# Two layers of cross attention on one core: nine slots for two units in place of ten, with maxima of up to 384 queries in a slot's four PSUM banks

## The chip, the cores and the metric

The kernel runs on one core of one Trainium2 chip. The metric is the device time of one execution in microseconds (us), and lower is better. All arithmetic is in fp32. The profile is of one execution on the same core.

## The reference, cut to what matters

Two cross-attention layers stand one behind the other. There are 32 batches of 256 queries with 320 channels, a context of 77 rows of 512 channels for each batch, and 20 heads of 16 channels. The context is so short that the object, adapter and image parts of the two original layers are empty; what is left is the same computation twice, with different weights:

```
q   = x @ Wq                    # (32, 256, 320)
k,v = ctx @ Wk, ctx @ Wv        # (32, 77, 320)
s   = q_h . k_h / 4             # per head h, 256 x 77
p   = softmax(s over the 77 keys)
x   = (merge_h(p @ v_h)) @ Wo + b + x
```

The second layer takes the x that the first has made.

## The kernel before, in words

**Layout.** Channels stand on partitions. A pair of batches (`NB = 2`) is one tile of x, 128 partitions by 1280 columns: channels 0 to 127 and 128 to 255 of both batches, and the last 64 channels of the two batches below each other. One pair in one layer is a *unit*; there are 32 units. `units_in_order` gives layer 0 of the first four pairs, and then layer 1 of a pair and layer 0 of a later pair in turn, so that from unit 4 on the even units are layer 1 and the odd ones layer 0.

**Groups.** The heads of a unit are worked on in five *groups* g of 256 queries (`of_group`): a group has eight heads of one batch, two in each of the four strips of 32 partitions (j = 0 to 3).

**Steps of a unit u**, each a function:

- `queries` with `queries_rest`, or, from unit 3 on, `outputs_and_queries(u - 3, u)`: the output projection of an older unit and the query projection of this one in one long step. Its results are added to x by VectorE (`add`, L520) and copied to the tile q0 by ScalarE (L369, L372), in the order rest, group 0, 1, 2, 3. A DMA copies q0 to q1.
- `keys(u, 0)`, `keys(u, 1)`, `keys_rest(u)`: the key projection, copied by ScalarE, masked for even and odd heads by GpSimd (`mask_keys`, tiles kT). `less_keys` makes the tile kM from the same keys.
- `vals` and `place_vals`: value projection in chunks of 128 context rows, copied by ScalarE and placed by DMA.
- `maxima(u, g)` (L423, tiles psm): the scores of the 256 queries of a group with all keys, queries on partitions. Each of the four strips has its own PSUM bank with 2 x 154 columns; VectorE reduces each bank to the maxima (L431). A call is 8 matmuls in the code, 16 in the profile[...].
- `turn(u)` (L440): VectorE transposes the maxima of the unit, and eight small DMAs write them into free rows of q0 and q1. These rows make the matmul of the scores take the maximum off.
- `scores(u, g)` (L458, tiles pss): keys on partitions, four banks of 512 columns, and ScalarE's exponential of each bank into a tile pT (L464).
- `values(u, g)` (L478, tile po): the product with the values, one bank; then `divide`: VectorE transposes the bank (L490) and takes reciprocals (L494), GpSimd multiplies (L499).
- `turn_back(u, g)` (L513): VectorE transposes the group back into the tile oT, from which the output projection reads.

Matmuls with 32 rows (psm, pss) use TensorE as four row tiles; those with 32 output channels (po and all projections) as four column tiles, and a few with 64 rows as eight tiles.

**Order.** All instructions are issued in an order written out by hand. `place` maps a slot number and a name to steps; the slots are walked one after the other, and in a slot the names in this order:

```
order = (
    "load", "maxima", "turn", "turn back", "scores", "values", "rest", "back", "full", "last",
)
```

Each engine works its instructions off in that order; only semaphores hold it up. Before, unit u has its groups in slots `NG * u` to `NG * u + 4`: one group of scores, one of values and one call of maxima in each slot, the long step `outputs_and_queries` in every fifth slot. PSUM has one pool of eight banks for everything (`bank`), which are given out in turn: a tile gets the bank of the tile eight allocations earlier, and has to wait until that one has been read. In the last units (`late`) the output projection is cut in two halves (`finish(u, (t,))`, which reads group 4 of oT first) and `finish_rest`, to fill slots that have no other work.

Of the kernel before, what the change touches and what calls it, by code (L numbers as in the profile page):

```python
# [52 lines left out]
B, S, C, CA, L = 32, 256, 320, 512, 77  # L56
HEADS, HD = 20, 16
P = 128
# [4 lines left out]
NG = 5  # L63
# [29 lines left out]
def xattn_kernel(ctx: ExitStack, tc: tile.TileContext, xT, cT, cP, weights, outT):  # L93
# [2 lines left out]
    const = ctx.enter_context(tc.tile_pool(name="const", bufs=1))  # L96
    io = ctx.enter_context(tc.tile_pool(name="io", bufs=3))
    work = ctx.enter_context(tc.tile_pool(name="work", bufs=3))
    probs = ctx.enter_context(tc.tile_pool(name="probs", bufs=8))
    psum = ctx.enter_context(tc.tile_pool(name="psum", bufs=8, space=bass.MemoryType.PSUM))  # L100

    units = units_in_order()
    NU = len(units)

    def bank(name):
        return psum.tile([P, 512], F32, tag="bank", name=name)
# [3 lines left out]
    def load_x(p):  # L110
        x_sb = io.tile([P, NX], F32, tag="x", name=f"x_{p}", bufs=AHEAD + 3)
        xs[p] = x_sb
        if p == 0:
            for a, b in ((0, NT), (NT, 2 * NT), (2 * NT, NX)):
                nc.sync.dma_start(out=x_sb[:, a:b], in_=xT[p, :, a:b])
        else:
            (nc.scalar if p == 1 else nc.sync).dma_start(out=x_sb, in_=xT[p])

    def load_context(u):
        p = units[u][0]  # L120
        c_sb = cs[u] = io.tile([P, NKA, NB * L], F32, tag="c", name=f"c_{u}", bufs=3)
        nc.sync.dma_start(out=c_sb, in_=cP[:, p])
# [18 lines left out]
    first, _, _ = PARTS["q"]  # L141
# [50 lines left out]
    def of_group(x, g):  # L192

        if g < 4:
            return x[:, (g // 2) * NT + (g % 2) * S : (g // 2) * NT + (g % 2 + 1) * S]
        return x[:, 2 * NT : NX]
# [75 lines left out]
    def keys(u, t):  # L272
        p, layer = units[u]
        w, c_sb = w_sb[layer], cs[u]
        if t == 0:
            st[u]["kr"] = work.tile([P, NG, L], F32, tag="kR", name=f"kR_{u}", bufs=2)
        kR = st[u]["kr"]
        ps = bank(f"psk_{u}_{t}")
        for kc in range(NKA):
            by_columns(  # L280
                ps[:, 0 : 2 * L],
                w["k"][:, kc, t * P : (t + 1) * P],
                c_sb[:, kc, :],
                start=(kc == 0),
                stop=(kc == NKA - 1),
            )
        nc.scalar.copy(kR[:, 2 * t : 2 * t + 2].rearrange("p g k -> p (g k)"), ps[:, 0 : 2 * L])  # L287
        mask_keys(u, t)

    def keys_rest(u):  # L290

        p, layer = units[u]
        w, c_sb = w_sb[layer], cs[u]
        ps = bank(f"psk_{u}_2")
        for kc in range(NKA):
            for i in range(4):
                b, m = 1 - i // 2, i % 2
                nc.tensor.matmul(  # L298
                    ps[32 * i : 32 * i + 32, 0:L],
                    w["k"][:, kc, 2 * P + 32 * m : 2 * P + 32 * m + 32],  # L300
                    c_sb[:, kc, b * L : (b + 1) * L],
                    start=(kc == 0),
                    stop=(kc == NKA - 1),
                )
        nc.scalar.copy(st[u]["kr"][:, 4], ps[:, 0:L])
        mask_keys(u, 2)
# [7 lines left out]
    def queries(u):  # L314

        p, layer = units[u]
        w = w_sb[layer]
        q0 = new_queries(u)
        ps = [[bank(f"psq_{u}_{t}_{b}") for b in range(NB)] for t in range(2)]
        if u == 0:  # L320

            main_channels(ps, w["q"], xs[p], start=True, stop=False)
            last_channels(ps, w["q2"], xs[p], start=False, stop=True)
        else:
            last_channels(ps, w["q2"], xs[p], start=True, stop=False)
            main_channels(ps, w["q"], xs[p], start=False, stop=True)
        for g in range(4):
            nc.scalar.copy(of_group(q0, g), ps[g // 2][g % 2][:, 0:S])

    def queries_rest(u):  # L330
        p, layer = units[u]
        w = w_sb[layer]
        q0, q1 = st[u]["q"]
        ps = bank(f"psq_{u}_2")
        project_rest(ps, w["q"], w["q22"], xs[p], swap=1)
        nc.scalar.copy(of_group(q0, 4), ps[:, 0:S])
        nc.sync.dma_start(out=q1, in_=q0)
# [75 lines left out]
                )  # L413


    def maxima(u, g):
        q0, kT, mx = st[u]["q"][0], st[u]["k", g // 2], maxes[u % 2]
        q = of_group(q0, g)
        ps = [bank(f"psm_{u}_{g}_{j}") for j in range(4)]
        for c in range(S // P):  # L420
            for j in range(4):
                r = slice(32 * j, 32 * j + 32)
                nc.tensor.matmul(  # L423
                    ps[j][:, c * 2 * L : (c + 1) * 2 * L],
                    q[r, c * P : (c + 1) * P],
                    kT[r, :, g % 2, :],
                    start=True,
                    stop=True,
                )
        for j in range(4):  # L430
            nc.vector.tensor_reduce(  # L431
                mx[:, 2 * g : 2 * g + 2, 2 * j : 2 * j + 2],
                ps[j][:, : 4 * L].rearrange("p (c e k) -> p c e k", e=2, k=L),
                AX.X,
                ALU.max,
            )
# [70 lines left out]
    def values(u, g):  # L507
        st[u]["n", g] = divide(u, g, products(u, g))
# [47 lines left out]
    def at(slot, where, step):  # L556
        place.setdefault((slot, where), []).append(step)

    end = NG * NU
    late = {
        NU - 4: (end - 10, end - 9, end - 8),
        NU - 3: (end - 7, end - 6, end - 5),
        NU - 2: (end - 4, end - 1, end - 3),
    }
    made = [0, 0]
    for u, (p, layer) in enumerate(units):
        s = NG * u
        if layer == 0 and u > 0:  # L570
            at(s - 15, "load", lambda p=p: load_x(p))
        if u > 0:
            at(s - 13, "load", lambda u=u: load_context(u))
        if u > 1:
            at(s - 9, "rest", lambda u=u: keys(u, 0))
            at(s - 9, "rest", lambda u=u: keys_rest(u))
            at(s - 8, "rest", lambda u=u: keys(u, 1))
        paired = u > 2 and u - 3 not in late
        if paired:
            at(s - 10, "full", lambda u=u: outputs_and_queries(u - 3, u))  # L580
        else:
            if u > 1:
                at(s - 10, "last", lambda u=u: queries(u))
            at(s - 6, "rest", lambda u=u: queries_rest(u))
        at(s - 6, "rest", lambda u=u: less_keys(u))
        need = range(p * NB * L // P, ((p + 1) * NB * L - 1) // P + 1)
        new = [i for i in need if i >= made[layer]]
        made[layer] += len(new)
        slots = {}
        for k, i in enumerate(new):  # L590
            at(s - 10 + k, "load", lambda layer=layer, i=i: load_chunk(layer, i))
            for h in range(2):
                slots[i] = s - 7 + (u == 0) + (k if len(new) > 1 else h)
                at(slots[i], "full", lambda layer=layer, i=i, h=h: vals(layer, i, h))
        for i in need:
            at(slots.get(i, s - 7), "full", lambda u=u, i=i: place_vals(u, i))
        for g in range(NG):
            if u > 0:
                at(s - 7 + g, "maxima", lambda u=u, g=g: maxima(u, g))
            at(s + g, "scores", lambda u=u, g=g: scores(u, g))  # L600
            at(s + g + 1, "values", lambda u=u, g=g: values(u, g))
            if g < 4:
                at(s + g + 2, "turn back", lambda u=u, g=g: turn_back(u, g))
            else:
                at(s + g + 1, "back", lambda u=u, g=g: turn_back(u, g))
        if u > 0:
            at(s - 3, "turn", lambda u=u: turn(u))
        if u == NU - 1:
            at(s + NG, "full", lambda u=u: finish(u))
            at(s + NG, "last", lambda u=u: finish_rest(u))  # L610
        if u in late:
            for t in range(2):
                at(late[u][t], "full", lambda u=u, t=t: finish(u, (t,)))
            at(late[u][2], "rest", lambda u=u: finish_rest(u))
            at(max(late[u]), "last", lambda u=u: store(u))
# [3 lines left out]
    for u, slot in ((0, -9), (1, -4)):  # L619
        for t in range(2):  # L620
            at(slot, "rest", lambda u=u, t=t: keys(u, t))
        at(slot, "rest", lambda u=u: keys_rest(u))
    for slot, g in ((-6, 0), (-5, 1), (-4, 2), (-4, 3), (-3, 4)):
        at(slot, "maxima", lambda g=g: maxima(0, g))
    at(-3, "turn", lambda: turn(0))
    at(-3, "last", lambda: queries(1))


    at(-10, "load", lambda: load_weights(0, "v", "v", nc.scalar))
# [108 lines left out]
```

## Time and profile before

| | |
|---|---|
| time, median of three executions | 961.7 us (961.33, 961.7, 3365.69) |
| the profiled execution: its time | 960.31 us |
| the profiled execution: span from first to last instruction | 958.5 us |
| granted TensorE clock | 1.000 |
| TensorE matmuls | 953.5 us busy, 20910 instructions |
| VectorE | 553.1 us busy, 1323 instructions |
| ScalarE | 435.6 us busy |
| GpSimd | 254.1 us busy |
| DMA | 83.77 MB, mean 87 GB/s |

The profile's ends of matmuls are modelled, so their durations overlap; what a phase of matmuls takes is read from the start of one phase to the start of the next. Where a fence shows lines of the timeline, the columns are start in us, duration in us, engine, line, operation, output and input tiles, shapes, number of instructions, and in brackets the idle time before with its releaser. Lines with "xcount" are groups: busy time, mean ns of one, idle time before and what ended it.

### The profile page before, as it was taken

Reading aid. Unit: us, or ns where it says so; the run is one execution under the profiler, and the core shown is the slowest. Engines: PE = TensorE matmul, PEld = TensorE weight load, DVE = VectorE, ACT = ScalarE, POOL = GpSimd, SP = SyncE. Lnnn points to the kernel's source line nnn. Section 1 sums busy time; section 2 is a strip of 40 time slices with the busy share of each in tenths; the row PEclk is TensorE's granted clock in tenths of the full one; section 3 lists DMA queues with packets and bytes.
Section 4 is the critical chain, followed back from the end, with each engine's and each line's share of the span. In section 5 each row is a group of like instructions: output and inputs, shape, how many; then the busy total and the mean of one; then the engine's idle time right before and its main releaser. Section 6 shows DMA issues by size and latency. Waiting matters only on the chain.

```text
span 958.5 us, 46529 instructions
## 1 busy us (share of the span) xinstructions
PE 953.5 (99%) x20910; PEld 628.8 (66%) x20910; DVE 553.1 (58%) x1323; ACT 435.6 (45%) x977; POOL 254.1 (27%) x422
## 2 busy tenths in 40 slices
PE   9999999999999999999999999999999999999998
PEld 7666766666666676666666666666667666667654
DVE  3456554666555665555665556655566555565664
ACT  2345544455444454444544444543445444445543
POOL 2223321333222332322332223322133222233311
PEclk9999999999999999999999999999999999999999
DMA  7533222131222222231222222322313122122102
GB/s 253 196 109 100 71 70 97 61 100 60 87 97 86 74 83 78 94 110 59 73 85 88 99 73 70 102 80 90 97 61 106 61 81 71 59 73 71 53 32 84
DMA packets 54537, 83.77 MB, mean 87 GB/s; under 512 B 15620, under 2 KB 36228, under 8 KB 54338
## 3 DMA queue, kind: packets, MB, share of 16 engines
q1 hardware_dynamic: 53386, 78.29, 25.1%
q8 instruction: 164, 2.69, 1.2%
q10 hardware_dynamic: 952, 2.50, 0.7%
q14 instruction: 35, 0.29, 0.1%
HBM read 35.39 MB, written 10.49 MB: 48 GB/s over the span
## 4 chain that ended last, share of the span: by engine, by line
PE 99%; issue 0%; DVE 0%
PE po L478 17%; PE psy L190 15%; PE psq L190 15%; PE pss L458 15%; PE psm L423 12%; PE psv L190 9%; PE psk L190 7%; PE psy L224 4%; PE psq L224 4%; PE psk L298 2%; PE warm L183 0%; DVE x L520 0%; DVE ones L150 0%
## 5 line engine op out<-in xcount | busy, mean ns | idle before, releaser
L464 ACT ACTIVATE pT<-pss 77x512 f32<-77x512 f32 x640 | 326.8, 590 | 216.4 <-PE pss L458 216.4
L431 DVE TENSOR_REDUCE max<-psm 128x4 f32<-128x308 f32 x640 | 261.5, 471 | 262.5 <-PE psm L423 262.3
L499 POOL TENSOR_TENSOR normal<-turned,inv 128x256 f32<-128x256 f32 x160 | 99.2, 620 | 678.8 <-DVE inv L494 678.8
L478 PE MATMUL po<-pT,v 77*32 77x256 f32 x2560 | 171.5, 385 | 0.0
L458 PE MATMUL pss<-q,kM 32*77 32x256 f32 x2560 | 167.1, 374 | 0.0
L190 PE MATMUL psy<-oT,w 128*32 128x256 f32 (+1 forms) x3072 | 164.4, 379 | 0.0
L190 PE MATMUL psq<-x,w 128*32 128x256 f32 (+1 forms) x3072 | 151.2, 379 | 0.0
L423 PE MATMUL psm<-kT,q 32*128 32x154 f32 x2560 | 129.6, 314 | 0.6 <-issue 0.6
L190 PEld LDWEIGHTS psy<-oT,w 128*32 128x32 f32 (+1 forms) x3072 | 88.3, 108 | 63.5 <-issue 16.1
L478 PEld LDWEIGHTS po<-pT,v 77*32 77x32 f32 x2560 | 67.0, 109 | 87.1 <-DVE max L431 56.8
L490 DVE STREAM_TRANSPOSE turned<-po 128x512 f32<-128x512 f32 x160 | 113.4, 709 | 15.3 <-PE po L478 15.3
L190 PEld LDWEIGHTS psq<-x,w 128*32 128x32 f32 (+1 forms) x3072 | 85.6, 109 | 54.0 <-issue 1.8
L423 PEld LDWEIGHTS psm<-kT,q 32*128 32x128 f32 x2560 | 92.3, 183 | 41.5 <-issue 29.5
L520 DVE SCALAR_TENSOR_TENSOR x<-psy,w,x 128x256 f32<-128x256 f32 x160 | 69.3, 478 | 81.6 <-PE psy L190 80.3
L261 POOL TENSOR_SCALAR kT<-kR,masks 128x154 f32<-128x154 f32 (+1 forms) x186 | 111.0, 612 | 9.4 <-ACT kR L287 9.4
L458 PEld LDWEIGHTS pss<-q,kM 32*77 32x77 f32 x2560 | 98.8, 141 | 19.8 <-issue 1.2
L190 PE MATMUL psv<-w,cv 128*32 128x160 f32 x2464 | 98.8, 299 | 0.0
L369 ACT COPY q<-psq 128x256 f32<-128x256 f32 x28 | 10.4, 372 | 184.5 <-PE psq L224 184.5
L190 PEld LDWEIGHTS psv<-w,cv 128*32 128x32 f32 x2464 | 82.4, 110 | 14.6 <-issue 0.5
L513 DVE STREAM_TRANSPOSE oT<-normal 128x256 f32<-128x256 f32 x160 | 68.9, 431 | 26.1 <-POOL normal L499 26.1
L190 PE MATMUL psk<-c,w 128*32 128x154 f32 x2048 | 78.8, 294 | 0.0
L190 PEld LDWEIGHTS psk<-c,w 128*32 128x32 f32 x2048 | 66.2, 110 | 11.8 <-DMA w<-in_w_dram 0.4
(31 smaller groups left out, 445.3 us busy)
## 6 DMA issues: line engine op xcount, KB each, us to landing
q<-q SPq DMA_DIRECT2D x32, 640.0 KB
c<-in_cP_dram SPq DMA_DIRECT2D x32, 308.0 KB
cv<-in_cT_dram SPq DMA_DIRECT2D x38, 256.0 KB
out_dram<-x SPq DMA_DIRECT2D x15, 640.0 KB
x<-in_xT_dram SPq DMA_DIRECT2D x14, 640.0 KB
v<-stage SPq DMA_DIRECT2D x26, 192.5 KB
q<-mT SPq DMA_DIRECT2D x254, 5.0 KB
w<-in_w_dram ACTq DMA_DIRECT2D x2, 640.0 KB
```

The source lines that it names most:

```text
L190: nc.tensor.matmul(out[m : m + 32], lhsT[:, m : m + 32], rhs, **flags)
L224: nc.tensor.matmul(ps[o : o + 32, 0:S], lhsT, rhs, **flags)
L261: engine.tensor_scalar_mul(kT[:, e], kR[:, groups], masks[:, e : e + 1])
L423: nc.tensor.matmul(ps[j][:, c * 2 * L : (c + 1) * 2 * L], q[r, c * P : (c + 1) * P], kT[r, :, g % 2, :], start=True, stop=True,)
L431: nc.vector.tensor_reduce(mx[:, 2 * g : 2 * g + 2, 2 * j : 2 * j + 2], ps[j][:, : 4 * L].rearrange("p (c e k) -> p c e k", e=2, k=L), AX.X ...
L458: nc.tensor.matmul(ps[j][:L, e * S : (e + 1) * S], kM[r, e, g, :], q[r, :], start=True, stop=True,)
L464: nc.scalar.activation(st[u]["p", g][j][:L], ps[j][:L], AF.Exp, scale=SCALE)
L478: nc.tensor.matmul(po[o : o + 32, e * S : (e + 1) * S], vpad[:L, b, pair, e].rearrange("p a d -> p (a d)"), pT[j][:L, e * S : (e + 1) * S] ...
L490: nc.vector.transpose(turned[:, 0 : 2 * S], po)
L499: nc.gpsimd.tensor_tensor(normal.rearrange("p q e d -> p e q d"), outs, inv.unsqueeze(3).broadcast_to([P, 2, S // 32, HD]), ALU.mult,)
L513: nc.vector.transpose(of_group(st[u]["o"], g), normal)
L520: nc.vector.scalar_tensor_tensor(x, ps[:, 0:S], w_sb[layer]["b"][:, 0, t : t + 1], x, ALU.add, ALU.add)
```

## The change

Two units, an even and the odd one behind it, now share nine slots in place of ten. `start(u)` is the first slot of a unit: 9k for the even unit 2k, 9k + 4 for the odd unit 2k + 1. The even unit has the scores of its groups 0 and 1 both in its first slot. `maxima` takes a run of 128-query pieces instead of a group: up to three of them (384 queries, 462 columns of a bank) go into one set of four banks and are reduced by one instruction per bank. A unit has four calls, of 1, 3, 3 and 3 pieces for an even unit and 3, 3, 2 and 2 for an odd one, in the four slots behind the slot of its query projection; that slot of an even unit has no maxima. The pool of the probabilities grows from 8 to 11 tiles. Keys, values, context and x loads, `turn` and the late outputs move with the new slots; unit 1 has all its maxima ahead of slot 0, where before they lay in slots -2 to 2.

For reference, the light work of the nine slots of a pair, with units 2k and 2k + 1 in scores and values and the next pair 2k + 2 and 2k + 3 in preparation:

| slot | maxima pieces | scores, group | values, group | projections |
|---|---|---|---|---|
| 9k | none | 2k: 0 and 1 | 2k-1: 4 | outputs 2k-1, queries 2k+2 |
| 9k+1 | 1 | 2k: 2 | 2k: 0 and 1 | keys_rest |
| 9k+2 | 3 | 2k: 3 | 2k: 2 | keys 0, vals |
| 9k+3 | 3 | 2k: 4 | 2k: 3 | keys 1, vals |
| 9k+4 | 3, then turn | 2k+1: 0 | 2k: 4 | outputs 2k, queries 2k+3 |
| 9k+5 | 3 | 2k+1: 1 | 2k+1: 0 | keys_rest, vals |
| 9k+6 | 3 | 2k+1: 2 | 2k+1: 1 | vals |
| 9k+7 | 2 | 2k+1: 3 | 2k+1: 2 | keys 0 |
| 9k+8 | 2, then turn | 2k+1: 4 | 2k+1: 3 | keys 1 |

```diff
-    probs = ctx.enter_context(tc.tile_pool(name="probs", bufs=8))
+    probs = ctx.enter_context(tc.tile_pool(name="probs", bufs=11))
...
-    def maxima(u, g):
-        q0, kT, mx = st[u]["q"][0], st[u]["k", g // 2], maxes[u % 2]
-        q = of_group(q0, g)
-        ps = [bank(f"psm_{u}_{g}_{j}") for j in range(4)]
-        for c in range(S // P):
+    def maxima(u, first, n):
+
+        q0, mx = st[u]["q"][0], maxes[u % 2]
+        ps = [bank(f"psm_{u}_{first}_{j}") for j in range(4)]
+        for i in range(n):
+            g, c = (first + i) // 2, (first + i) % 2
+            q, kT = of_group(q0, g), st[u]["k", g // 2]
             for j in range(4):
                 r = slice(32 * j, 32 * j + 32)
                 nc.tensor.matmul(
-                    ps[j][:, c * 2 * L : (c + 1) * 2 * L],
+                    ps[j][:, i * 2 * L : (i + 1) * 2 * L],
...
             nc.vector.tensor_reduce(
-                mx[:, 2 * g : 2 * g + 2, 2 * j : 2 * j + 2],
-                ps[j][:, : 4 * L].rearrange("p (c e k) -> p c e k", e=2, k=L),
+                mx[:, first : first + n, 2 * j : 2 * j + 2],
+                ps[j][:, : n * 2 * L].rearrange("p (c e k) -> p c e k", e=2, k=L),
...
+    def start(u):
+
+        return 9 * (u // 2) + 4 * (u % 2)
+
+    def slot_of(u, g):
+        return start(u) + (g if u % 2 else max(0, g - 1))
...
-    end = NG * NU
+    end = start(NU)
     late = {
-        NU - 4: (end - 10, end - 9, end - 8),
-        NU - 3: (end - 7, end - 6, end - 5),
+        NU - 4: (end - 11, end - 10, end - 9),
+        NU - 3: (end - 9, end - 8, end - 7),
         NU - 2: (end - 4, end - 1, end - 3),
     }
...
-        s = NG * u
+        s = start(u - 2)
         if layer == 0 and u > 0:
-            at(s - 15, "load", lambda p=p: load_x(p))
+            at(s - 5, "load", lambda p=p: load_x(p))
         if u > 0:
-            at(s - 13, "load", lambda u=u: load_context(u))
+            at(s - 4, "load", lambda u=u: load_context(u))
         if u > 1:
-            at(s - 9, "rest", lambda u=u: keys(u, 0))
-            at(s - 9, "rest", lambda u=u: keys_rest(u))
-            at(s - 8, "rest", lambda u=u: keys(u, 1))
+            at(s - 2, "rest", lambda u=u: keys(u, 0))
+            at(s - 1, "rest", lambda u=u: keys(u, 1))
+            at(s + 1, "rest", lambda u=u: keys_rest(u))
         paired = u > 2 and u - 3 not in late
         if paired:
-            at(s - 10, "full", lambda u=u: outputs_and_queries(u - 3, u))
-        else:
-            if u > 1:
-                at(s - 10, "last", lambda u=u: queries(u))
-            at(s - 6, "rest", lambda u=u: queries_rest(u))
-        at(s - 6, "rest", lambda u=u: less_keys(u))
+            at(s, "full", lambda u=u: outputs_and_queries(u - 3, u))
+        elif u > 1:
+            at(s, "last", lambda u=u: queries(u))
+            at(s, "last", lambda u=u: queries_rest(u))
+        if u > 1:
+            at(s + 2, "rest", lambda u=u: less_keys(u))
...
+        first = (-6, -2, s + 2, s + 1)[u if u < 2 else 2 + u % 2]
...
+        h = 0
+        for k, n in enumerate((3, 3, 2, 2) if u % 2 else (1, 3, 3, 3)):
+            if u > 1:
+                at(s + 1 + k, "maxima", lambda u=u, h=h, n=n: maxima(u, h, n))
+            h += n
+        if u > 1:
+            at(s + 4, "turn", lambda u=u: turn(u))
         for g in range(NG):
-            if u > 0:
-                at(s - 7 + g, "maxima", lambda u=u, g=g: maxima(u, g))
-            at(s + g, "scores", lambda u=u, g=g: scores(u, g))
-            at(s + g + 1, "values", lambda u=u, g=g: values(u, g))
+            slot = slot_of(u, g)
+            at(slot, "scores", lambda u=u, g=g: scores(u, g))
+            at(slot + 1, "values", lambda u=u, g=g: values(u, g))
             if g < 4:
-                at(s + g + 2, "turn back", lambda u=u, g=g: turn_back(u, g))
+                at(slot + 2, "turn back", lambda u=u, g=g: turn_back(u, g))
             else:
-                at(s + g + 1, "back", lambda u=u, g=g: turn_back(u, g))
-        if u > 0:
-            at(s - 3, "turn", lambda u=u: turn(u))
+                at(slot + 1, "back", lambda u=u, g=g: turn_back(u, g))
...
     at(-3, "turn", lambda: turn(0))
     at(-3, "last", lambda: queries(1))
+    at(-2, "rest", lambda: queries_rest(1))
+    for slot, h, n in ((-2, 0, 3), (-1, 3, 3), (-1, 6, 2), (-1, 8, 2)):
+        at(slot, "maxima", lambda h=h, n=n: maxima(1, h, n))
+    at(-1, "turn", lambda: turn(1))
```

More of the change, by code (lines that the diff above doesn't have):

```diff
@@ L588, in xattn_kernel @@
         made[layer] += len(new)
+        first = (-6, -2, s + 2, s + 1)[u if u < 2 else 2 + u % 2]
         slots = {}
         for k, i in enumerate(new):
-            at(s - 10 + k, "load", lambda layer=layer, i=i: load_chunk(layer, i))
+            at(first - 3 + k, "load", lambda layer=layer, i=i: load_chunk(layer, i))
             for h in range(2):
-                slots[i] = s - 7 + (u == 0) + (k if len(new) > 1 else h)
+                slots[i] = first + (k if len(new) > 1 else h)
                 at(slots[i], "full", lambda layer=layer, i=i, h=h: vals(layer, i, h))
         for i in need:
-            at(slots.get(i, s - 7), "full", lambda u=u, i=i: place_vals(u, i))
+            at(slots.get(i, first), "full", lambda u=u, i=i: place_vals(u, i))
+        h = 0
[5 more added lines that the diff above has]
+            at(s + 4, "turn", lambda u=u: turn(u))
         for g in range(NG):
-            if u > 0:
-                at(s - 7 + g, "maxima", lambda u=u, g=g: maxima(u, g))
-            at(s + g, "scores", lambda u=u, g=g: scores(u, g))
-            at(s + g + 1, "values", lambda u=u, g=g: values(u, g))
+            slot = slot_of(u, g)
+            at(slot, "scores", lambda u=u, g=g: scores(u, g))
+            at(slot + 1, "values", lambda u=u, g=g: values(u, g))
             if g < 4:
-                at(s + g + 2, "turn back", lambda u=u, g=g: turn_back(u, g))
+                at(slot + 2, "turn back", lambda u=u, g=g: turn_back(u, g))
             else:
-                at(s + g + 1, "back", lambda u=u, g=g: turn_back(u, g))
-        if u > 0:
-            at(s - 3, "turn", lambda u=u: turn(u))
+                at(slot + 1, "back", lambda u=u, g=g: turn_back(u, g))
         if u == NU - 1:
-            at(s + NG, "full", lambda u=u: finish(u))
-            at(s + NG, "last", lambda u=u: finish_rest(u))
+            at(end, "full", lambda u=u: finish(u))
+            at(end, "last", lambda u=u: finish_rest(u))
         if u in late:
@@ L622, in xattn_kernel @@
         at(slot, "rest", lambda u=u: keys_rest(u))
+        at(slot, "rest", lambda u=u: less_keys(u))
+    at(-6, "rest", lambda: queries_rest(0))
     for slot, g in ((-6, 0), (-5, 1), (-4, 2), (-4, 3), (-3, 4)):
-        at(slot, "maxima", lambda g=g: maxima(0, g))
+        at(slot, "maxima", lambda g=g: maxima(0, 2 * g, 2))
     at(-3, "turn", lambda: turn(0))
     at(-3, "last", lambda: queries(1))
+    at(-2, "rest", lambda: queries_rest(1))
+    for slot, h, n in ((-2, 0, 3), (-1, 3, 3), (-1, 6, 2), (-1, 8, 2)):
+        at(slot, "maxima", lambda h=h, n=n: maxima(1, h, n))
+    at(-1, "turn", lambda: turn(1))
     at(-10, "load", lambda: load_weights(0, "v", "v", nc.scalar))
```

## The prediction

> **What bounds the kernel now.** I read the page's busy times and its chain first, then the matmuls' timeline in the middle of the run, and then the other engines around the long step.
>
> ```profile
> PE 953.5 (99%) x20910; PEld 628.8 (66%) x20910; DVE 553.1 (58%) x1323; ACT 435.6 (45%) x977; POOL 254.1 (27%) x422
> PE 99%; issue 0%; DVE 0%
> ```
>
> TensorE is 99% of the span and 99% of the chain that ended last: nothing else pays unless TensorE gets less to do or starts to wait. The change takes no matmul away, so I need to know what lies between them. One slot of the timeline, and the next slot's start:
>
> ```profile
> 492.46 1.24 PE L190 MATMUL psk<-c,w 128*32 128x154 f32 x32
> 493.63 0.81 PE L423 MATMUL psm<-kT,q 32*128 32x154 f32 x16
> 494.26 1.04 PE L458 MATMUL pss<-q,kM 32*77 32x256 f32 x16
> 495.23 1.07 PE L478 MATMUL po<-pT,v 77*32 77x256 f32 x16
> 496.12 1.27 PE L190 MATMUL psv<-w,cv 128*32 128x160 f32 x32
> 497.32 0.81 PE L423 MATMUL psm<-kT,q 32*128 32x154 f32 x16
> ...
> 501.02 0.81 PE L423 MATMUL psm<-kT,q 32*128 32x154 f32 x16
> 501.65 1.04 PE L458 MATMUL pss<-q,kM 32*77 32x256 f32 x16
> 502.62 1.07 PE L478 MATMUL po<-pT,v 77*32 77x256 f32 x16
> 503.51 3.64 PE L190 MATMUL psy<-oT,w 128*32 128x256 f32 x64
> 506.96 1.05 PE L224 MATMUL psy<-oT,w 128*32 128x256 f32 x16
> ```
>
> The reader is to see start-to-start times: psm 0.63, pss 0.97, po 0.89, psv 1.20. Four tiles run side by side, so x64 is 16 waves: 3.45 / 16 = 0.216 us for a wave of 256 columns, and four waves are 0.86. The pss phase takes 0.11 more before po can follow, po 0.03 more. Inside one tiling, 32 psk matmuls take 1.06 to the next key matmuls (488.27 to 489.33) and 1.17 where psm follows: 0.11 to 0.14 on leaving the column tiles. A wave of 154 columns is 1.06 / 8 = 0.13, so psm's 0.63 is 0.52 of waves and 0.11 on entering. Where pss comes first in the row tiles, it takes 1.03 (921.52 to 922.55) and not 0.97: 0.06 on entering.
>
> The other engines around the long step:
>
> ```profile
> 485.50 0.80 ACT L372 COPY q<-psq 128x256 f32<-128x256 f32 x2 [0.92 <-PE psq L190]
> 485.78 0.81 PE L423 MATMUL psm<-kT,q 32*128 32x154 f32 x16
> 486.42 1.04 PE L458 MATMUL pss<-q,kM 32*77 32x256 f32 x16
> ...
> 492.47 0.51 DVE L440 STREAM_TRANSPOSE mT<-max 128x320 f32<-128x320 f32 x1
> 492.90 0.40 DVE L513 STREAM_TRANSPOSE oT<-normal 128x256 f32<-128x256 f32 x1
> ...
> 501.84 1.64 DVE L431 TENSOR_REDUCE max<-psm 128x4 f32<-128x308 f32 x4 [0.77 <-PE psm L423]
> 503.39 0.43 DVE L513 STREAM_TRANSPOSE oT<-normal 128x256 f32<-128x256 f32 x1
> 503.76 0.72 DVE L490 STREAM_TRANSPOSE turned<-po 128x512 f32<-128x512 f32 x1
> ```
>
> The last query copy ends at 486.30, 0.52 after the long step, and psm covers that; group 3 of oT is ready at 503.82, 1.0 us before TensorE wants it. Both margins are touched by the change.
>
> **What the Trainium skill says.** TensorEngine Tiling (Array Packing), Key Properties: a change of tiling mode drains TensorE. The trace agrees, with the 0.11 and 0.11 to 0.14 above. Perfetto Trace Analysis, Tensor Engine Instruction: a matmul's recorded end is computed, not seen; here psm "ends" at 494.44 with pss started at 494.26, so I use starts. VectorE: DVE Perf Modes, perf-mode tier table and Specifications: `tensor_reduce` has only the 1x mode, at 0.96 GHz; 154 more columns then cost 0.16 us, an estimate. The trace has no reduction of another length, but its transposes give 709 - 431 ns for 256 columns, 1.09 ns each, near it. PSUM — Partial Sum Buffer, Specifications (TRN2): eight banks of 512 fp32; three pieces (462 columns) fit, a fourth would not.
>
> **Gains.** (1) 144 slots replace 160. Each slot less saves one leave of the row tiles (0.11), one entry of po (0.03) and one leave of the column tiles (0.13): 16 x 0.27 = 4.3 us. (2) Calls of maxima: five a unit before, 159 separate entries (two of unit 0 lie together). After: four a unit, 120 for units 2 to 31, and unit 1's last three lie together: 126. 33 x 0.11 = 3.6 us. (3) 17 more slots begin their row tiles with pss: 17 x 0.06 = -1.0 us. Sum: -6.9 us. Moved loads cost nothing while they land in time: in the middle of the run the q copy and the context load issued at 486.33 and 486.92 are through by 491, and the shortest new lead, the even unit's context from slot 9k+5 to its keys in 9k+7, is about 10 us.
>
> **VectorE's and ScalarE's cover.** A reduction of 308 columns takes a step of 0.39 (501.84 to 503.39 for four); of 462 then 0.55; four end 2.28 after the first start. Fewer of them save VectorE time that nobody waits for. With three pieces, TensorE's light slot is 0.89 + 0.97 + 0.89 + projections, 4.0 to 5.0 us; VectorE's 2.2 + 0.4 + 0.7 + 0.25 = 3.6, so it keeps up. Tightest: the transposed po of slot 9k+6 is due free as a bank for pss in 9k+7 at 4.56 and is read by 4.42. The eight exponentials of slot 9k (0.51 each) start 1.06 after it begins and free their banks in time for po (due 1.8, free 1.6), and for y one bank every 0.51. A fourth pT of group 1 reuses a tile of group 4 of the unit before, whose po is through by then. These I cost at nothing.
>
> **New waits.** (a) Slot 9k+1. Its pss takes the four banks of the query copies. Psm there has one piece, 0.37 in place of 0.63; the fourth bank is free at 0.52 + 0.06 after the long step, pss wants it at 0.37. The in-order TensorE queue behind it (po, keys) waits too: 0.22, 15 times: 3.3 us. Bounds: 0.15 to 0.27. (b) Slot 9k+4. Three pieces, then `turn`, then oT of group 3, all in one VectorE queue, ahead of the long step that reads that group in its fourth block. First reduction 1.08 after the slot's start (0.82 before, plus 0.26), all done at 3.36, `turn` to 3.82 (0.43, and it waits for the last maximum), oT at 4.22, seen by TensorE at 4.29. TensorE is there at 0.89 + 0.97 + 0.89 + 3 x 0.43 = 4.02. 0.27, 14 times: 3.8 us. Bounds: nothing, if a reduction of 462 is 0.48; 0.6, if it is 0.63. (c) Start. Unit 1's maxima in slot -1 are three calls in a row with 12 banks. The last takes the banks of the first, whose reductions come 0.55 apart: 1.9 us. The `queries(2)` behind two groups of scores waits for banks that exponentials free every 0.51, one group more than before: 1.0. (d) End. `finish(29, (0,))` now stands in the slot of group 4 of the same unit. From the start of po to oT there were 3.39 us (942.68 to 946.07: po, transpose, reciprocal, GpSimd, transpose); with `finish_rest(28)` between, TensorE is there after 0.89 + 1.28 = 2.17: 1.3 us. `finish(30, (0,))` likewise, one bare slot between: 0.5. Bare slots 138 to 140 wait for exponentials: 0.2. Sum of (a) to (d): 12.0 us.
>
> **Sum.** -6.9 + 12.0 = +5.1 us against the profiled execution's 960.3: 965.4. The median shown, 961.7, is 1.4 above that execution; with it 966.5, 0.5% above before. The measure tells about 2% from no change, so this reads as the same.
>
> **The rivals.**
> *The waits are covered.* If (a) and (b) fail to appear, because the copies end earlier or the long reduction is cheap, -6.9 + 4.9 (c, d) = -2.0: 959.5. For it: both margins are tenths of a us, worked out from rows of other shapes. Against it: the orders of VectorE, ScalarE and TensorE are fixed and each term has a duration in the trace.
> *VectorE's long reductions set the pace.* One mechanism: 20 pieces a pair are reduced in 32 instructions, 20 of them of 462 columns, a length that no row shows. From 0.58 each on, slot 9k+7's pss waits for po's bank as well as (b) growing; four reductions in a row make four times the excess. At 0.70, (b) grows by 4 x 0.15 = 0.6 and 9k+7 waits 4 x 0.12 = 0.5, 14 times each: 966.5 + 15 = 982, slower. For it: the single 308-column reduction is recorded at 469 ns, more than its step of 0.39, so a fixed part is hidden by overlap. Against it: the 1.09 ns a column of the transposes.
> *It doesn't shorten the row phases.* If psm's 0.11 on entry is a rate (128 weight columns a piece, 183 ns a load beside waves of 0.13) and not an entry, gain (2) is gone: 966.5 + 3.6 = 970. Against it: in the x32 psm phase at 20.14 the starts of waves lie 0.13 apart after a first of 0.23.
>
> **How the numbers follow.** Forecast, waits and gains as summed (with the lost entry of the third rival counted to it): 0.64, and it spans 962 to 971. Waits covered: 0.24, 955 to 962. Long reductions: 0.12, 971 to 990. The range 957 to 974 leaves out the low end of the second and most of the third, about 2 in 10. Faster by over 2% (below 942.5) would need three times the whole gain: 0.01. Slower by over 2% (above 980.9) is the upper half of the long reductions and what I have not seen: 0.06. Within 2%: 0.93.
>
> **What would show it.** Right: psm entries 126; psm start-to-start about 0.37, 0.63 and 0.89 for 1, 2 and 3 pieces; pss in slot 9k+1 about 1.2 in place of 0.97; the first psy phase of slot 9k+4 about 3.7 in place of 3.45; reductions of 462 columns 0.55 apart; a long psm phase near 36 us. Wrong: idle TensorE in slots 9k+2, 9k+3 or 9k+5 to 9k+8, or q, c or v DMAs as releasers of TensorE.

## The result and the profile after

The changed kernel takes 968.4 us in the median of its executions, the kernel before 961.3 us: a ratio of 1.0067, 95% interval 1.0052 to 1.0082. The forecast was 966.5 us with a range of 957 to 974. The loss is real and small: 7 us, under the 2% that count as a difference here.

The first recorded profile of the changed kernel fell into an execution with a TensorE clock of 0.655 throughout (1376 us), so the profile read here is of the same kernel run again, 968.38 us, with a span of 966.6 us. That run measured a ratio of 1.0065 (1.0053 to 1.0078).

The page's busy times and its chain:

```profile
PE 958.9 (99%) x20910; PEld 632.7 (65%) x20910; DVE 539.7 (56%) x1199; ACT 432.4 (45%) x977; POOL 254.1 (26%) x422
PE 94%; DVE 4%; DMA 1%; issue 0%; ACT 0%; POOL 0%; DVEq 0%; POOLq 0%
PE po L481 15%; PE psq L191 15%; PE pss L461 14%; PE psy L191 13%; PE psm L426 11%; PE psv L191 9%; PE psk L191 7%; PE psy L225 4%; PE psq L225 4%; DVE max L434 3%; PE psk L299 2%; DVE mT L443 1%; DVE oT L516 1%; DMA w<-in_w_dram 0%; DMA v<-stage 0%
```

The busy line hardly moves: TensorE still reads 99%, since a matmul that waits is recorded as a longer one (the psy phase below as 3.91 us, and as 3.64 where it does not wait). The chain tells what that hides. Before, it was TensorE for 99%; now 4% of it is VectorE, and the lines name the maxima (L434), the turn (L443) and the transpose back (L516), the three steps of wait (b). The 1% of DMA is the first load of weights and three steps of a copy of values, which the chain puts in the middle of reductions that run without a gap in the timeline. VectorE itself has become less busy (553.1 to 539.7 us), and has entered the chain all the same.

Wait (b) in the timeline, a slot 9k+4. Its pieces of maxima begin at 480.32, its long step at 483.07:

```profile
481.41 2.28 DVE L434 TENSOR_REDUCE max<-psm 128x6 f32<-128x462 f32 x4 [1.49 <-PE psm L426]
...
483.07 3.91 PE L191 MATMUL psy<-oT,w 128*32 128x256 f32 x64
483.72 0.51 DVE L443 STREAM_TRANSPOSE mT<-max 128x320 f32<-128x320 f32 x1
484.15 0.40 DVE L516 STREAM_TRANSPOSE oT<-normal 128x256 f32<-128x256 f32 x1
...
486.80 1.05 PE L225 MATMUL psy<-oT,w 128*32 128x256 f32 x16
```

The reductions run from 1.09 to 3.37 after the slot's start, the turn follows when the last is through, and the transpose of group 3 ends at 484.55, 4.23 after the slot's start. The forecast had 1.08, 3.36 and 4.22. The psy phase takes 3.73 from start to start in place of 3.45: the whole long step takes 11.48 (483.07 to 494.55) against 11.21 in the next one, which has no such wait (513.51 to 524.72).

Wait (a), a slot 9k+1:

```profile
524.43 0.80 ACT L373 COPY q<-psq 128x256 f32<-128x256 f32 x2 [0.92 <-PE psq L191]
524.72 0.55 PE L426 MATMUL psm<-kT,q 32*128 32x154 f32 x8
525.09 1.29 PE L461 MATMUL pss<-q,kM 32*77 32x256 f32 x16
525.28 0.99 DVE L434 TENSOR_REDUCE max<-psm 128x2 f32<-128x154 f32 x4 [4.47 <-PE psm L426]
...
526.30 1.93 PE L481 MATMUL po<-pT,v 77*32 77x256 f32 x32
```

One piece covers 0.37, from 524.72 to 525.09. The last of the query copies, whose banks pss takes, ends at 525.23, and pss takes 1.21 from start to start in place of 0.97.

VectorE's reductions by shape (the columns are busy us, mean ns of one, idle time before):

```profile
L434 DVE TENSOR_REDUCE max<-psm 128x6 f32<-128x462 f32 x308 | 175.3, 631 | 158.2 <-PE psm L426 158.2
L434 DVE TENSOR_REDUCE max<-psm 128x4 f32<-128x308 f32 x148 | 60.3, 471 | 22.8 <-PE psm L426 22.7
L434 DVE TENSOR_REDUCE max<-psm 128x2 f32<-128x154 f32 x60 | 14.9, 310 | 73.0 <-PE psm L426 73.0
```

154 more columns cost 160 ns twice over. That agrees with the estimate of 0.16 us, which the prediction worked out from the 0.96 GHz that the Trainium skill gives for VectorE (VectorE: DVE Perf Modes, Specifications). Four reductions of 462 columns end 2.28 after the first start, which is a step of 0.55, where the rival of costly long reductions needed 0.58 or more; it is out. Psm took 0.37, 0.63 and 0.90 for one, two and three pieces. The second and the third piece add 0.26 and 0.27, so 0.11 is left as an entry and is not a rate; that rival is out as well.

At the start, the burst of unit 1's maxima in slot -1:

```profile
34.96 1.60 PE L426 MATMUL psm<-kT,q 32*128 32x154 f32 x40
...
36.05 5.36 DVE L434 TENSOR_REDUCE max<-psm 128x6 f32<-128x462 f32 x12 [2.37 <-PE psm L426]
36.84 2.33 PE L426 MATMUL psm<-kT,q 32*128 32x154 f32 x16 [0.28 <-DVE max L434]
39.10 2.08 PE L191 MATMUL psk<-c,w 128*32 128x154 f32 x32
40.95 2.17 PE L191 MATMUL psv<-w,cv 128*32 128x160 f32 x32
...
43.05 1.97 PE L461 MATMUL pss<-q,kM 32*77 32x256 f32 x32
```

The seven pieces take 4.14, for 0.11 + 14 x 0.13 + 0.12 = 2.05 of work: 2.1 of waiting, 1.9 forecast. What I had not foreseen are the next two phases: 1.85 for keys that take 1.07 elsewhere and 2.10 for values that take 1.20. The timeline names no wait inside them; the granted clock says why (busy us of each engine, then PEclk, DMA share and GB/s, in stretches of 2 us):

```profile
36.00:38.00 2.00, 1.70 (x25) 1.07 (x18) 1.95 (x4) 0.00 (x0) 0.00 (x0) 1.00 0.85 292
38.00:40.00 2.00, 1.98 (x32) 1.48 (x36) 2.00 (x6) 0.00 (x0) 0.00 (x0) 0.84 0.96 271
40.00:42.00 2.00, 2.00 (x36) 1.63 (x32) 1.93 (x5) 0.29 (x1) 0.38 (x1) 0.50 0.69 251
42.00:44.00 2.00, 2.00 (x40) 1.38 (x36) 0.00 (x0) 0.29 (x1) 0.94 (x2) 0.81 0.05 15
```

The clock falls to 0.50 from the end of the burst on and costs (1.85 - 1.07) + (2.10 - 1.20) = 1.7 us. The clock column gives the same: 0.32 + 1.00 + 0.38 = 1.7 us lost, which at half the clock is a fall of 3.4 us. Three of the five executions of this run have a mean clock of 0.998 (968.4 to 968.7 us); the other two, at 0.999 and 1.000, took 966.4 and 966.9.

At the end, wait (d), the half output of unit 29 in the slot of its own group 4:

```profile
923.35 1.48 PE L225 MATMUL psy<-oT,w 128*32 128x256 f32 x24
926.02 2.53 PE L191 MATMUL psy<-oT,w 64*32 64x256 f32 x48 [1.19 <-DVE oT L516]
```

These are the 1.28 us of `finish_rest` and then 1.4 us of waiting for the transpose, 1.3 forecast.

### The profile page after: what moved, and what is told of

It reads as the page before. It is cut to its first block, busy times and chain, and to the rows that moved or that the text cites. A ratio compares the mean times of both kernels' runs of the same rounds, so it can differ in the third digit from the quotient of the medians.

```text
span 1374.5 us, 46485 instructions
## 1 busy us (share of the span) xinstructions
PE 1369.2 (100%) x20910; PEld 727.2 (53%) x20910; DVE 549.7 (40%) x1199; ACT 436.9 (32%) x977; POOL 256.0 (19%) x422
## 4 chain that ended last, share of the span: by engine, by line
PE 100%; DVE 0%; issue 0%
PE po L481 16%; PE psy L191 16%; PE pss L461 15%; PE psq L191 15%; PE psm L426 10%; PE psv L191 10%; PE psk L191 7%; PE psy L225 4%; PE psq L225 4%; PE psk L299 2%; PE warm L184 0%; DVE x L523 0%; DVE oT L516 0%; DVE ones L151 0%
## 5 line engine op out<-in xcount | busy, mean ns | idle before, releaser
L434 DVE TENSOR_REDUCE max<-psm 128x6 f32<-128x462 f32 (+2 forms) x516 | 250.4, 548 | 479.7 <-PE psm L426 479.7
L191 PE MATMUL psy<-oT,w 128*32 128x256 f32 (+1 forms) x3072 | 238.4, 509 | 1.1 <-DVE oT L516 1.1
L461 PE MATMUL pss<-q,kM 32*77 32x256 f32 x2560 | 235.8, 509 | 0.0
L481 PE MATMUL po<-pT,v 77*32 77x256 f32 x2560 | 229.6, 504 | 0.0
L191 PE MATMUL psq<-x,w 128*32 128x256 f32 (+1 forms) x3072 | 223.2, 511 | 0.0
L426 PE MATMUL psm<-kT,q 32*128 32x154 f32 x2560 | 152.8, 361 | 0.0
L191 PE MATMUL psv<-w,cv 128*32 128x160 f32 x2464 | 143.0, 385 | 0.0
L426 PEld LDWEIGHTS psm<-kT,q 32*128 32x128 f32 x2560 | 111.6, 221 | 54.2 <-issue 47.3
L262 POOL TENSOR_SCALAR kT<-kR,masks 128x154 f32<-128x154 f32 x186 | 112.2, 615 | 37.9 <-ACT kR L288 35.6
L191 PE MATMUL psk<-c,w 128*32 128x154 f32 x2048 | 113.9, 381 | 0.0
L370 ACT COPY q<-psq 128x256 f32<-128x256 f32 x28 | 10.4, 373 | 287.8 <-PE psq L225 287.8
L225 PE MATMUL psy<-oT,w 128*32 128x256 f32 (+1 forms) x768 | 95.0, 511 | 0.0
L225 PE MATMUL psq<-x,w 128*32 128x256 f32 (+1 forms) x768 | 94.9, 501 | 0.0
```

Source lines behind the costliest of these rows:

```text
L191: nc.tensor.matmul(out[m : m + 32], lhsT[:, m : m + 32], rhs, **flags)
L225: nc.tensor.matmul(ps[o : o + 32, 0:S], lhsT, rhs, **flags)
L262: engine.tensor_scalar_mul(kT[:, e], kR[:, groups], masks[:, e : e + 1])
L426: nc.tensor.matmul(ps[j][:, i * 2 * L : (i + 1) * 2 * L], q[r, c * P : (c + 1) * P], kT[r, :, g % 2, :], start=True, stop=True,)
L434: nc.vector.tensor_reduce(mx[:, first : first + n, 2 * j : 2 * j + 2], ps[j][:, : n * 2 * L].rearrange("p (c e k) -> p c e k", e=2, k=L), ...
L461: nc.tensor.matmul(ps[j][:L, e * S : (e + 1) * S], kM[r, e, g, :], q[r, :], start=True, stop=True,)
```

## The experiments

Each run has a ratio to the kernel before on the same chip. Three chips were used: one for the changed kernel again and its two single edits and their pair, a second for the next four runs, a third for the last two. The kernel before took 961.16, 961.07 and 960.72 us on them, so a difference from the changed kernel's 968.38 that crosses chips is uncertain by up to half a us. There are five executions of each kernel, but 15 of "Both" and 21 each of the two pieces and of the ten slots.

The fall of the clock splits the executions in two, so differences are also given between executions of the same kind. "Kept the clock" is a mean of 0.999 or 1.000 and "lost it" one of 0.998. The changed kernel's five have a mean time of 966.7 us where they kept it (two) and 968.5 where they lost it (three).

**The changed kernel again.** No edit.

> The changed kernel as it is, for a profile at full clock. The forecast's steps (gains 6.9 us, waits 12.0 us): 966.5 us; psm entries 126, psm 0.37, 0.63 and 0.89 us from start to next phase for one, two and three pieces; pss in slot 9k+1 near 1.2 us; the first psy phase of slot 9k+4 near 3.7 us; reductions of 462 columns 0.55 us apart. If the waits are covered: 959.5 us with pss 0.97 and psy 3.45 there. If long reductions set the pace: reductions 0.70 us apart and pss late in slot 9k+7 too. If psm's entry is a rate: psm 0.94 us for three pieces and 0.32 for one. A fourth theory after the result, that the lower granted clock (0.998 in the record of the times) carries part of the loss: up to 2 us, to be seen as slices of lower clock.

Measured: 968.38 us. The points of the forecast's list came: 126 psm phases (159 before); psm 0.37, 0.63, 0.90; pss 1.21 or 1.22 in all 15 slots 9k+1; psy 3.72 or 3.73 in all 14 slots 9k+4; and no TensorE wait in slots 9k+7 and 9k+8. One thing came that the forecast had named as a sign of being wrong: in one slot 9k+6, at 501.79, the values took 1.63 in place of 1.20. Two neighbouring units, between the starts behind their long steps, take 28.22 + 29.75 = 57.97 us (524.72 to 582.69), before 28.92 + 28.93 = 57.85. So a pair loses 0.1 us, where it would gain 0.4 without the waits; the rest of the loss lies at the two ends.

**Two pieces ahead of the scores in slot 9k+1.**

```diff
-        for k, n in enumerate((3, 3, 2, 2) if u % 2 else (1, 3, 3, 3)):
+        for k, n in enumerate((3, 3, 2, 2) if u % 2 else (2, 3, 2, 3)):
```

> Even units take 2, 3, 2 and 3 pieces in their four calls in place of 1, 3, 3 and 3; all else as in the changed kernel. Slot 9k+1 then has two pieces, 0.63 us, ahead of its pss, and 9k+4 still has three. If wait (a) is real: 15 x 0.22 = 3.3 us faster than the changed kernel, pss there 0.97. If the waits are covered: no difference. If long reductions set the pace: no difference in 9k+1, a little less in 9k+4's neighbour, under 1 us.

Measured: 962.89 us, ratio 1.0025 (1.0018 to 1.0032). Its slot 9k+1:

```profile
520.45 0.80 ACT L373 COPY q<-psq 128x256 f32<-128x256 f32 x2 [0.92 <-PE psq L191]
520.73 0.81 PE L426 MATMUL psm<-kT,q 32*128 32x154 f32 x16
521.37 1.04 PE L461 MATMUL pss<-q,kM 32*77 32x256 f32 x16
...
522.34 1.93 PE L481 MATMUL po<-pT,v 77*32 77x256 f32 x32
```

The copies end 0.52 after the long step as before, two pieces cover 0.64, and pss is back at 0.97. The long step of slot 9k+4 stays at 11.47, and a pair takes 57.72, 0.25 less. The median gains 5.5 us, more than 3.3. Executions that kept the clock gain 4.0, those that lost it 3.6. So wait (a) is real, 0.25 x 15 = 3.7 us; the rest of the median's gain is that 12 of these 21 executions kept the clock and only two of the changed kernel's five.

**Transpose back ahead of the turn.**

```diff
-        "load", "maxima", "turn", "turn back", "scores", "values", "rest", "back", "full", "last",
+        "load", "maxima", "turn back", "turn", "scores", "values", "rest", "back", "full", "last",
```

> The steps 'turn back' of a slot come ahead of 'turn' in VectorE's order, in all slots; all else as in the changed kernel. Group 3 of oT is then ready 0.46 us earlier in slot 9k+4, at 3.8 of 4.02. If wait (b) is real: 14 x 0.27 = 3.8 us faster than the changed kernel, psy there 3.45. If the waits are covered: no difference. If reductions of 462 columns are 0.70 us apart: the wait was 0.87 and 0.41 of it stay, 6.4 us faster.

Measured: 964.70 us, ratio 1.0036 (1.0023 to 1.0048), 3.7 us less than the changed kernel in the median. Its slot 9k+4:

```profile
482.59 3.64 PE L191 MATMUL psy<-oT,w 128*32 128x256 f32 x64
483.12 0.43 DVE L516 STREAM_TRANSPOSE oT<-normal 128x256 f32<-128x256 f32 x1
483.48 0.47 DVE L443 STREAM_TRANSPOSE mT<-max 128x320 f32<-128x320 f32 x1
...
486.05 1.05 PE L225 MATMUL psy<-oT,w 128*32 128x256 f32 x16
```

The psy phase is back at 3.46, all long steps take 11.20 or 11.21, and pss in slot 9k+1 stays at 1.22. The executions that kept the clock gain 2.6 us and those that lost it 3.0, but these are two and three executions. Wait (b) is real, near the forecast's 3.8 (14 x 0.27 in the trace), and made by the order of two instructions in VectorE's queue.

**Both.**

> Both edits: 2, 3, 2 and 3 pieces for even units, and 'turn back' ahead of 'turn'. If (a) and (b) are separate waits: 3.3 + 3.8 = 7.1 us faster than the changed kernel, near the time before (961). If one hides behind the other: less than the sum of the two single edits. If the waits are covered: no difference.

Measured: 960.27 us, ratio 0.9986 (0.9978 to 0.9993), 8.1 us less than the changed kernel in the median, against 7.1 expected; 7.1 less among the executions that kept the clock (nine) and 7.6 among those that lost it (six). The two waits add up. Slot 9k+4 of this kernel:

```profile
477.59 2.28 DVE L434 TENSOR_REDUCE max<-psm 128x6 f32<-128x462 f32 x4 [2.08 <-PE psm L426]
...
479.26 3.64 PE L191 MATMUL psy<-oT,w 128*32 128x256 f32 x64
479.79 0.43 DVE L516 STREAM_TRANSPOSE oT<-normal 128x256 f32<-128x256 f32 x1
480.15 0.47 DVE L443 STREAM_TRANSPOSE mT<-max 128x320 f32<-128x320 f32 x1
...
482.71 1.05 PE L225 MATMUL psy<-oT,w 128*32 128x256 f32 x16
```

and its chain:

```profile
PE 99%; DVE 0%; issue 0%; POOL 0%; POOLq 0%
```

Group 3 is turned back by 480.22. TensorE comes to it after three blocks of 0.43, at about 480.55, and VectorE has left the chain. A pair takes 27.71 + 29.75 = 57.46, 0.39 less than before: the gain of a slot saved, 0.43 in the forecast, without its waits.

**Unit 1's maxima spread over slots -2 to 1.**

```diff
-    for slot, h, n in ((-2, 0, 3), (-1, 3, 3), (-1, 6, 2), (-1, 8, 2)):
+    for slot, h, n in ((-2, 0, 3), (-1, 3, 3), (0, 6, 2), (1, 8, 2)):
         at(slot, "maxima", lambda h=h, n=n: maxima(1, h, n))
-    at(-1, "turn", lambda: turn(1))
+    at(1, "turn", lambda: turn(1))
```

> Unit 1's last two calls of maxima lie in slots 0 and 1 in place of slot -1, and its 'turn' in slot 1; all else as in the changed kernel. If wait (c) is real: the psm burst of slot -1 (4.1 us in the changed kernel's trace for work of 2.0) goes, 2 us faster, less up to 0.6 for pss that may wait in slot 0. If the fall of the granted clock to 0.50 behind that burst comes from TensorE standing idle in it: no execution shows a clock under 0.999, and those of the changed kernel that fell (0.998, 1.7 us longer) are the ones that gain most, so the median gains 3 to 4 us. If the clock falls for another reason: executions of 0.998 stay.

Measured: 964.81 us, ratio 1.0039 (1.0026 to 1.0051), 3.6 less than the changed kernel in the median and 1.9 less than its executions that kept the clock; all five executions here show a clock of 1.000. The burst is gone, but the scores of slot 0 take 2.89 in place of 1.90, and in slot 1 three pieces and the scores take 2.63 where 1.87 is usual. I had expected up to 0.6 of such waiting. The 1.0 of slot 0 is no loss of its own, though: `queries(2)` behind it takes 0.9 less than in the changed kernel, so this wait has only moved. The waits fit that the moved maxima hold banks which the scores want; no run takes this apart.

**The late outputs one slot back.**

```diff
-        NU - 3: (end - 9, end - 8, end - 7),
-        NU - 2: (end - 4, end - 1, end - 3),
+        NU - 3: (end - 8, end - 7, end - 6),
+        NU - 2: (end - 3, end - 1, end - 2),
```

> The late outputs of units 29 and 30 move one slot back (29 to end - 8, - 7, - 6; 30 to end - 3, - 1, - 2); all else as in the changed kernel. If wait (d) is real: the 1.3 us before finish(29, (0,)) and the 0.5 before finish(30, (0,)) go, and bare slots that wait for exponentials cost 0.2 to 0.4 more: 1.4 to 1.6 us faster than the changed kernel. If the ends are hidden anyway: no difference.

Measured: 965.73 us, ratio 1.0046 (1.0032 to 1.0060). The median gains 2.7 us, but four of the five executions kept the clock, against two of five; these four lie at 964.8 to 965.8 against 966.4 to 966.9, about 1.2 less, on another chip. The trace has the parts: the phase of `finish_rest` takes 1.41 in place of 2.67, the 0.46 ahead of unit 30's output is gone, and a bare slot waits 0.24 more (po 1.42 in place of 1.18), 1.5 in all. Wait (d) agrees, with an uncertainty as large as a third of it.

**All four edits.**

> All four edits: 2, 3, 2 and 3 pieces for even units, 'turn back' ahead of 'turn', unit 1's maxima spread, the late outputs one slot back. If the waits (a) to (d) are the whole loss, only the gains are left: 12 us faster than the forecast of 966.5, 954.5 to 956 us, 0.6% faster than before. If something else costs: it stays near the 960.3 of the two edits together.

Measured: 958.31 us, ratio 0.9968 (0.9956 to 0.9981). Faster than before, yet 2 to 4 us short of what was expected. The waits that the spread of unit 1's maxima brings with it are in its trace: pss takes 2.17 in slot 1 in place of 0.97, 1.2 us of loss, and 2.89 in slot 0, which `queries(2)` gives back as above.

**Maxima in four calls, in the ten slots of before.** The function `maxima` of the change in the kernel before, with this placement:

```diff
-        for g in range(NG):
-            if u > 0:
-                at(s - 7 + g, "maxima", lambda u=u, g=g: maxima(u, g))
+        h = 0
+        for k, n in enumerate((3, 3, 2, 2)):
+            if u > 0:
+                at(s - 7 + (k if k < 2 else k + 1), "maxima", lambda u=u, h=h, n=n: maxima(u, h, n))
+            h += n
```

> The kernel before with its ten slots, in which units from 1 on take their maxima in four calls of 3, 3, 2 and 2 pieces (in the slots of groups 0, 1, 3 and 4, so that the slot of the long step has none); slots, keys, loads and outputs as before. If psm's 0.11 is paid on entering: 31 x (0.11 - 0.06) = 1.6 us faster than before. If it is a rate: 31 x 0.06 = 1.9 us slower. If the long reductions hurt by themselves: slower, with TensorE waiting behind them.

Measured: 959.31 us, ratio 0.9982 (0.9975 to 0.9988), 1.8 us faster than before, 1.6 expected. Its slots with and without maxima:

```profile
497.86 1.07 PE L425 MATMUL psm<-kT,q 32*128 32x154 f32 x24
498.76 1.04 PE L460 MATMUL pss<-q,kM 32*77 32x256 f32 x16
499.73 1.07 PE L480 MATMUL po<-pT,v 77*32 77x256 f32 x16
501.82 1.10 PE L460 MATMUL pss<-q,kM 32*77 32x256 f32 x16
502.85 1.07 PE L480 MATMUL po<-pT,v 77*32 77x256 f32 x16
```

Three pieces take 0.90, and pss without maxima ahead of it 1.03 in place of 0.97. One part of the change, the longer calls of maxima, gains when taken alone; what the changed kernel loses, it loses by what its new slots put next to each other.

**Another start.** The four calls stay in slots -2 and -1, at the start and at the end of each:

```diff
-    for slot, h, n in ((-2, 0, 3), (-1, 3, 3), (-1, 6, 2), (-1, 8, 2)):
-        at(slot, "maxima", lambda h=h, n=n: maxima(1, h, n))
-    at(-1, "turn", lambda: turn(1))
+    for slot, where, h, n in (
+        (-2, "maxima", 0, 3), (-2, "last", 3, 3), (-1, "maxima", 6, 2), (-1, "last", 8, 2),
+    ):
+        at(slot, where, lambda h=h, n=n: maxima(1, h, n))
+    at(-1, "last", lambda: turn(1))
```

> The four calls of unit 1's maxima stay in slots -2 and -1, but stand in pairs at the start and at the end of them, with key and value projections between the second and third; 'turn' of unit 1 behind the last. All else as in the changed kernel. If the burst's wait for banks and the fall of the clock behind it are the loss at the start: the psm phases there lose their 2.1 us, no execution shows a clock under 0.999, one round of tilings more costs 0.3; scores of slot 0 may wait up to 1 us for banks that the last call holds. 1 to 2 us faster than the changed kernel's executions at full clock (966.4 to 966.9), 964.5 to 965.9, and 2.5 to 4 us faster than its median. If the clock falls for another reason: executions near 967.5 with 0.998 stay.

Measured: 965.32 us, ratio 1.0044 (1.0030 to 1.0058), as expected; the clock is 1.000 in all five executions again, and the same stretch of the run reads:

```profile
36.00:38.00 2.00, 1.81 (x60) 1.58 (x56) 1.28 (x3) 0.10 (x1) 0.00 (x0) 1.00 0.88 337
38.00:40.00 2.00, 2.00 (x61) 1.70 (x55) 2.00 (x5) 0.41 (x2) 0.89 (x2) 1.00 0.79 218
40.00:42.00 2.00, 2.00 (x37) 1.64 (x31) 2.00 (x6) 0.70 (x3) 0.44 (x1) 1.00 0.96 308
```

The DMA traffic is like that beside the fall (337, 218 and 308 GB/s against 292, 271 and 251), and the clock stays. There are now two different ways of taking the burst apart, with ten executions and no fall, but on other chips than the changed kernel's.

**All edits with this start.**

> The combination of the four edits with the start of e_c2 in place of e_c's, whose scores of slots 0 and 1 waited 2.2 us. If those waits were what kept the combination at 958.3: 956.5 to 957.5. If they were hidden behind something at the start: 958.3 again.

Measured: 956.00 us, ratio 0.9949 (0.9936 to 0.9962): half a per cent faster than before, and 12 us faster than the changed kernel (10.4 by the mean of the executions that kept the clock). It is 2.3 us below the combination before it, where 0.8 to 1.8 was expected and the chips differ by 0.35. In slot 1 pss is back at 0.97; in slot 0 the scores still wait. The 2.2 us of waiting that the expectation takes for the spread alone are those of the combination; in the spread alone it is 1.8.

## Why the prediction was right

The time, 968.4 for 966.5, and its sign came out of the sum of two numbers, the gains and the waits, and both held. In the order of the forecast:

- **Gains, 6.9 forecast.** The pair of both edits shows 0.39 where 6.9 / 16 = 0.43 was forecast, so about 6.2 over 16 pairs. The entry of psm (0.11) and the entry of a lone pss (0.06) are each seen directly, in the phases of 1, 2 and 3 pieces and in the ten-slot experiment. The 0.27 for a slot saved is seen only within the 0.39.
- **(a), 3.3 forecast:** 0.25 a pair, 3.7. Undone alone, gone.
- **(b), 3.8 forecast:** 0.28 a pair, 14 times, 3.9. Undone alone, 3.7 in the medians and 2.6 to 3.0 among like executions.
- **(c), 2.9 forecast:** 2.1 in the burst. The 1.0 for `queries(2)` wasn't tried by itself: that step with its rest took 6.77 in the changed kernel and 5.91 where one call of maxima lies ahead of the scores, but there the scores wait in its place. From the first score of slot 0 to the end of that step it is 8.67 in the changed kernel and 8.80 with the maxima spread, so no run has taken this wait away. The term missed the fall of the clock behind the burst, 1.7 in three of five executions, and is the mis-sized term of the sum: executions that kept the clock took 966.4 and 966.9.
- **(d), 2.0 forecast:** 1.4 for unit 29 and 0.5 for unit 30 (po of slot 140 takes 1.46 where 1.00 is usual) and 0.2 one slot ahead of it.

That the two times lie so close is in part chance. The forecast set its loss of 5.1 us on a median of 961.7, and in the 35 executions beside the changed kernel the kernel before took 961.2. The loss itself is 7.2 in the medians and 5.4 where the clock was kept. The terms as measured here sum to 12.7 - 6.2 = 6.5, so about 1 us of them is not accounted for.

The rivals: covered waits are refuted by the two single edits (their forecast, by its own sum of -2.0 on 961.7, should read 959.7 and not 959.5); costly long reductions by 631 - 471 = 160 ns and the step of 0.55; psm's entry as a rate by 0.37, 0.63 and 0.90. From slot 0 on the trace names no copy of q, context or values as what TensorE waited for. The one long values phase of a slot 9k+6, 0.43 too long, comes back in the same slot of three of the eight other traces with nine slots (1.62, 1.46 and 1.74), with no releaser that the profile shows; its cause stays open.

## What to carry to other kernels

Where one engine is the whole chain and its work doesn't change, a new order gains what it saves between the pieces of work, here tenths of a us a slot, and each wait that it opens costs as much; so count both lists before judging. Look first at the places where a covering step was shortened (one piece in place of two ahead of the scores) or where something was put into another engine's queue ahead of what the bound engine reads next (the turn ahead of the transpose back). An engine need not be busy to be on the chain: VectorE did less work after the change and appeared in it, and the order of two of its instructions was worth about 3 to 4 us.

## What the runs showed of the hardware

TensorE's granted clock fell to 0.50 for about 3.4 us behind a burst of some 4 us in which it waited half of the time for VectorE, in three of five executions of the changed kernel. A wait of 2 us then cost another 1.7 us behind it. By the mean clock of 0.998, the runs whose kernel has this burst lost the clock in 21 of 46 executions on one chip and in one of five on a second. With the burst taken apart, none of 20 executions lost it, ten on the second chip and ten on a third; nor did any of the 35 of the kernel before on the first.

That the waiting causes the fall fits all of this, but it isn't shown. No kernel without the burst but with the new slots ran on the chip where the clock fell most. And the burst alone does not decide: the trace with two pieces ahead of the scores has the same burst (1.70 us busy of 2.00 from 36 to 38, as in the changed kernel) and the clock stays at 1.00. How much waiting it takes wasn't measured.
